# Moving one VectorE step ahead of a PSUM eviction in a modulated convolution kernel

## The chip, the cores and the metric

The kernel runs on one core of one Trainium2 chip. The metric is the device time of one execution in microseconds. The core's engines work side by side, each through its own queue in order: TensorE (PE, matmuls; its weight loads are listed as PEld), VectorE (DVE), ScalarE (ACT), GpSimd (POOL) and SyncE (SP, which issues most of the transfers). They wait for one another by semaphores.

## The reference

The input is x, 128 samples of 64 channels and 1024 positions, and a style vector of 128 numbers for each sample. Four convolution layers (64 to 64 channels, 3 taps) follow one another, each with weights of its own for each sample, and the result is added to x:

```python
TYPES = ('same', 'upsample', 'same', 'downsample')

def _layer(x, style, w, b, mw, mb, typ):
    s = style @ mw.T + mb
    weight = SCALE * w * s[:, None, :, None]
    demod = lax.rsqrt(jnp.sum(weight * weight, axis=(2, 3)) + EPS)
    weight = weight * demod[:, :, None, None]
    if typ == 'same':
        out = jax.vmap(_conv_same)(x, weight) + b[None, :, None]
    elif typ == 'upsample':
        out = jax.vmap(_conv_up)(x, weight.transpose(0, 2, 1, 3)) + b[None, :, None]
        out = _blur(out, 2.0 * blur_k, (1, 1))
    elif typ == 'downsample':
        xb = _blur(x, blur_k, (2, 2))
        out = jax.vmap(_conv_down)(xb, weight) + b[None, :, None]
    return out
...
out = x
for i, typ in enumerate(TYPES):
    out = _layer(out, style, weights[i], biases[i], mod_w[i], mod_b[i], typ)
return x + out
```

There is no nonlinearity between the layers, so for each sample the four of them are one convolution.

## The kernel before, in words

**Composing the taps.** The kernel doesn't run four layers over the data. For each sample it multiplies the four layers' weights into the nine taps of one convolution, and runs that over x. Samples come in groups of four; there are 32 groups, numbered q. The composition of one group is a chain of small matmuls with PSUM evictions between them:

- `scale3` (ScalarE) makes `wd`, the last layer's weights with the group's factors.
- Stage 1 (`stage1_a`, `stage1_b`) multiplies `wd` with the third layer's weights into the PSUM tile `psS`. ScalarE evicts one part into the SBUF tile S in `stage1_a`. In `stage1_b` VectorE evicts the rest with two instructions (line 481), and GpSimd then adds two slots of S (line 484). This is what "the eviction of S" means below: the two VectorE instructions.
- `share_sums` (VectorE), `share` (TensorE) and `share_copy` (ScalarE, line 529) prepare stage 2 of a group one turn ahead: three products that several taps have in common are made in a corner of another PSUM tile and copied into the PSUM tile `psR`.
- Stage 2 (`stage2_rest`, matmuls on line 506) adds the rest onto `psR`; ScalarE evicts it into R.
- Stage 3 makes the weights `Wf`; `combine_a` and `combine_b` (VectorE) make from them the weights H of a fast convolution.

`psS`, `psR` and the `psW` of stage 3 live in the pool `ps_w`, which has one buffer of two banks: each of them can be written only when the one before has been read.

**The convolution.** Three planes of x (each third position) make five data products, a fast convolution with five products in place of more. The inputs of the products are sums of planes: VectorE makes G from x in two steps, the third plane (`in_g2`, 684 elements a partition) and the first two planes (`in_g01`, 1376 elements); T1 and T2 are a sum and a difference of planes of G, made by GpSimd (`in1`, line 776, and `in2`, line 781); T04 (`in04`) and T3 (`in3`, line 761) are made by VectorE. TensorE's `conv0` to `conv4` multiply them with the weights into the PSUM tiles `psA` (two buffers) and Y; `sum1` and `sum2` (VectorE, which reads `psA` into y and writes Y) combine the products; `output` (ScalarE) scales, adds the bias and writes the tile o, which SyncE stores.

**The order.** It is written out by hand: each engine runs its instructions in the order in which the functions are called. A turn works on several groups at once: q is finished, n = q + 1 is in the middle of its convolution, c = q + 2 gets its inputs G, T1 and T3 and its stage 3, c + 1 its share, and s = q + 4 its stage 1. Turns 0 to 3 are `early_turn`, 4 to 28 are `turn_of`, and the last groups are written out singly. `sharing(q)` holds for q = 5 to 27.

`side(SIDE, q)` is work on the edges of the samples, spread over the turns: in most turns one VectorE instruction (as `add0`, `add2`, `blur_side`), in some several small ones (`setup0` in turn 10, `setup1` in 13, `setup3` in 15, `rest1_edges` in 18), and none in turns 14 and 19. `slot` is TensorE work on the edges, in turns 10, 14, 15 and 19.

Of the kernel before, what the change touches and what calls it, by code (L numbers as in the profile page):

```python
# [63 lines left out]
def kernel(  # L64
# [76 lines left out]
    def load(q, planes=slice(0, 3), cs=range(2)):  # L141

        if q < NQ:
            at = slice(planes.start * PL, planes.stop * PL)
            for c in cs:
                nc.sync.dma_start(Xs[q % NX][:, c, at], x[2 * q + c, :, at])
# [314 lines left out]
    def stage1_a(q, ps=None):  # L461

        ps = ps or unit(ps_w, f"psS{q}")
        wd = chain[q]
        tap_matmul(ps, wd, 2, 2, w2n[:, 0, :], EVEN, first=True)
        tap_matmul(ps, wd, 3, 2, w2n[:, 2, :], EVEN)
        tap_matmul(ps, wd, 1, 1, w2n[:, 1, :], slice(1, 2))
        st, t = s_tiles(q)
        for r in range(2):
            scaled_copy(nc_a, flat(st[r][:, :4]), ps[r][:, C : 5 * C], tBn[:, q, r : r + 1])  # L470
        chain[q] = wd, ps, st, t
# [88 lines left out]
    def stage2(q, pool=None, engs=(nc_a, nc_a), between=None):  # L560
        if q in shared_ps:
            ps = stage2_rest(q)
        else:
            ps = opened.pop(q, None)
            taps = range(9) if ps is None else range(3, 9)
            ps = stage2_taps(q, taps, ps or unit(pool or ps_w, f"psR{q}"))
        if between:
            between()
        t = r_pool.tile([P, 2, 9, C], F32, tag="R", name=f"R{q}")
        for r in range(2):  # L570
            scaled_copy(engs[r], flat(t[:, r, :7]), ps[r][:, : 7 * C], tC[:, q, r : r + 1])
        chain[q] = t
        return ps
# [62 lines left out]
    def r_sums(q, eng):  # L636
        t = chain[q]
        eng.tensor_add(t[:, :, 7:9], t[:, :, 2:6:3], t[:, :, 3:7:3])
# [3 lines left out]
    def stage3_b(q, ps):  # L642

        new_w(q)
        t = chain[q]
        plan = (
            (slice(0, 3), w0s[2][:, 2, :], slice(0, 7, 3)),
            (slice(0, 2), w0s[2][:, 1, :], slice(1, 5, 3)),
            (slice(0, 2), w0s[2][:, 0, :], slice(2, 6, 3)),
            (slice(3, 4), w0s[0][:, 0, :], slice(0, 1)),  # L650
            (slice(4, 5), w0s[1][:, 0, :], slice(1, 2)),
            (slice(4, 5), w0s[1][:, 1, :], slice(0, 1)),
            (slice(5, 7), w0s[0][:, 1, :], slice(7, 9)),
        )
        for i, (at, weight, slots) in enumerate(plan):
            same_row(blocks(ps, at), weight, t, slots, i == 0, i == len(plan) - 1)
        pw = shared_w[q] = unit(ps_w, f"psW{q}")
        src = blocks(ps, slice(5, 7))
        for i, f in enumerate((1.0, 1.0 / 3.0)):
            for dst, v in zip(blocks(pw, slice(i, i + 3, 2)), src):  # L660
                scaled_copy(nc_a, dst, v, f)
        stage3_out(q, ps, 0, 5)

    def stage3_a(q):

        t, pw = chain[q], shared_w.pop(q)
        plan = (
            (slice(0, 3, 2), Wd[:, 0], slice(3, 7, 3)),
            (slice(0, 3, 2), w0s[0][:, 2, :], slice(1, 5, 3)),
            (slice(1, 4, 2), Wd[:, 1], slice(2, 6, 3)),  # L670
            (slice(1, 2), w0s[1][:, 0, :], slice(4, 5)),
        )
        for i, (at, weight, slots) in enumerate(plan):
            same_row(blocks(pw, at), weight, t, slots, last=i == len(plan) - 1)
        stage3_out(q, pw, 5, 4)
# [35 lines left out]
    def sum_of(out, x, f, y, op=ALU.add):  # L711
        nc_v.scalar_tensor_tensor(out, x, f, y, op0=ALU.mult, op1=op)  # L712
# [6 lines left out]
    def combine_a(q):  # L719

        chain.pop(q)
        a, b, c, h1, h2, h3 = taps(q)
        sum_of(h1, c, -2.0, a)
        residual(q)
        sum_of(h3, h1, 1.0 / 6.0, b)

    def combine_b(q, steps=range(3)):

        a, b, c, h1, h2, h3 = taps(q)
        plan = (h2, c, -0.5, a), (h1, b, -3.0, h2, ALU.subtract), (h2, h2, -1.0 / 3.0, b)  # L730
        for i in steps:
            sum_of(*plan[i])
# [10 lines left out]
    def plane(buf, i, pairs=BOTH_PAIRS):  # L743

        at = PL * (2 - i) if i < 3 else PL * 2 + 1
        return buf[:, pairs, at : at + NJ]
# [6 lines left out]
    def g_tile(q):  # L753
        if q not in Gs:
            Gs[q] = gpool.tile([P, 2, 3 * PL], F32, tag="G", name=f"G{q}")
        return Xs[q % NX], Gs[q]
# [6 lines left out]
    def in_g01(q, pairs=BOTH_PAIRS):  # L763
        if q < NQ:
            X, g = g_tile(q)
            sum_of(g[:, pairs, PL:], X[:, pairs, : 2 * PL], 0.5, X[:, pairs, PL:], ALU.subtract)

    def in_g2(q, pairs=BOTH_PAIRS):
        if q < NQ:
            X, g = g_tile(q)  # L770
            sum_of(plane(g, 2, pairs), plane(X, 3, pairs), 0.5, plane(X, 2, pairs), ALU.subtract)
# [6 lines left out]
    def in2(q, eng):  # L778
        if q < NQ:
            t, g = t_tile(q, "T12"), Gs[q]  # L780
            eng.tensor_sub(t[:, :, 1, :NJ], plane(g, 2), plane(g, 1))  # L781
# [46 lines left out]
    def open_a(q):  # L828
        A[q] = ps_conv.tile([P, 2, 512], F32, tag="u", name=f"psA{q}")
        return banks(q)  # L830

    def conv3(q, pool=None):
        if pool:
            A[q] = unit(pool, f"psA{q}")
        elif q not in A:
            open_a(q)
        product(q, 3, banks(q))

    def copy_m3(q):
        m3c[q] = m_tile("m3", q)  # L840
        for s, a in parts(q):
            nc_a.copy(m3c[q][:, s], a)
# [10 lines left out]
    def conv2(q, *groups):  # L853
        product(q, 2, banks(q), groups or range(K))

    def sum2(q, steps=(0, 1)):
        if 0 in steps:
            m3 = m3c.pop(q)
            for s, a in enumerate(banks(q)):
                sum_of(Y[:, s, :NB], m3[:, s], 3.0, a[:, :NB])  # L860
        for s, a in parts(q) if 1 in steps else ():
            nc_v.tensor_sub(y1w[q][:, s], y1w[q][:, s], a)

    def conv4(q, *groups):
        product(q, 4, Y_banks, groups or range(K))

    def conv0(q, *groups):
        product(q, 0, banks(q), groups)
# [409 lines left out]
    def high(n):  # L1278
        return Y[:, 1, NB + 4 : NB + 4 + n]
# [84 lines left out]
    def side(work, q):  # L1364
        work.get(q, lambda: None)()
# [4 lines left out]
    def sharing(q):  # L1370
        return FIRST < q < NQ - 4
# [111 lines left out]
    def turn_of(q):  # L1483
        n, c, s = q + 1, q + 2, q + 4
        entry = q == FIRST
        stage2(c)
        if entry:
            sum2(q)
            conv4(q)
            combine_a(n)  # L1490
            r_sums(c, nc_v)
        else:
            conv2(q)
            r_sums(c, nc_g)
            sum2(q)
            in2(n, nc_g)
        side(TABLES, q)
        for i in range(3):
            load(c + 1, slice(i, i + 1))
        stage3_b(c, open_a(n))  # L1500
        if entry:
            conv0(q, 0, 1)
        else:
            combine_a(n)
            conv4(q)
        stage3_a(c)
        combine_b(n)
        conv3(n)
        if entry:
            copy_m3(n)  # L1510
            stage1_a(s)
        outputs(q, 2)
        if not entry:
            if s < NQ:
                stage1_a(s)
            copy_m3(n)
        in04(n)
        if sharing(q):
            share_sums(c + 1)
        in_g2(c)  # L1520
        side(SIDE, q)
        if q in SMALL:
            l, bs = SMALL[q]
            nc_v.memset(high(bs.stop - bs.start), 0.0)
        conv0(q, *((2,) if entry else range(K)))
        if entry:
            conv1(n, 0, 1)
        outputs(q, 1)
        if s < NQ:
            stage1_b(s)  # L1530
        in_g01(c)
        if sharing(q):
            share(c + 1, banks(q))
            share_copy(c + 1)
        outputs(q, 0)
        if q in SLOTS:
            matmuls, width, rest = SLOTS[q]
            slot(matmuls, width, Y_banks)
            rest()
        if s == NQ:  # L1540
            slot(ends3, 3, unit(ps_w, "psE"), 3)
            rest3()
        conv1(n, *((2,) if entry else range(K)))
        if q in SMALL:
            small(q)
        sum1(n)
        in3(c)
        side(LATE, q)
        if s == NQ:
            in04(c)  # L1550
        in1(c, nc_g)
        if s + 1 < NQ:
            scale3(s + 1)
# [6 lines left out]
    q, n, c = NQ - 3, NQ - 2, NQ - 1  # L1560
# [161 lines left out]
```

## Time and profile before

| what | value |
|---|---|
| median of three runs | 476.29 us (475.52 to 476.63) |
| span of the profiled execution, first to last instruction | 475.5 us |
| TensorE busy | 469.7 us, 99% |
| VectorE busy | 417.3 us, 88% |
| ScalarE busy | 312.0 us, 66% |
| GpSimd busy | 165.8 us, 35% |
| granted TensorE clock | 0.998 |

The profile gives the span as the profiled execution's own time; no other time of that execution is recorded. A page of the profile lists busy times, the span in slices, the DMA queues, the chain of waits that ended last, and groups of instructions. A row of the timeline reads: start in us from the span's start, duration in us (of all instructions of the row, where "x2" or more are merged), engine, line of the kernel, operation, tile written and tiles read, shapes, and in brackets the idle time of the engine before it with what ended that. A row of the waits reads: the waiting engine, tile and line, what it waited for, the total in us, how many times, the longest.

### The profile page before, as it was taken

To read this page: it belongs to the slowest core of one execution; us is meant where nothing else is said; L and a number is where in the kernel's file an instruction comes from. 1 tells how busy PE (TensorE), PEld (TensorE's weight loads), DVE (VectorE), ACT (ScalarE), POOL (GpSimd) and SP (SyncE) were. 2 spreads that over 40 slices of the span, in tenths; PEclk is the share of its full clock that TensorE was granted. 3 is DMA by queue.
4 is the path that set the end of the run, shared out by engine and by line. 5 is a ranking of instruction groups with operands and counts; after the bars stand their busy time and mean duration, and the time that the engine had idled before them with its cause. 6 is when DMAs were issued, how large, how long until landed. Compare 5 with 4: busy or idle time off the path is not lost.

```text
span 475.5 us, 26771 instructions
## 1 busy us (share of the span) xinstructions
PE 469.7 (99%) x11932; PEld 349.5 (74%) x11932; DVE 417.3 (88%) x694; ACT 312.0 (66%) x711; POOL 165.8 (35%) x200
## 2 busy tenths in 40 slices
PE   9999999999999999999999999999999999999996
PEld 6987788777678876677776677766788787876653
DVE  3889998879989998899979899979998999999896
ACT  4565657577766676766667666667666777766464
POOL 3634033664444342233432233422333423243200
PEclk9999999999999999999999999999999999999999
DMA  5237456535445554345544454543555544455225
GB/s 176 71 115 224 150 151 180 152 113 177 139 145 166 166 166 136 123 150 169 163 150 126 130 168 152 178 124 121 152 164 169 164 145 147 148 152 161 80 91 193
DMA packets 52707, 70.71 MB, mean 149 GB/s; under 512 B 6000, under 2 KB 50672, under 8 KB 52592
## 3 DMA queue, kind: packets, MB, share of 16 engines
q1 hardware_dynamic: 52368, 68.78, 46.3%
q8 instruction: 93, 1.52, 1.4%
q10 hardware_dynamic: 224, 0.22, 0.1%
q14 instruction: 22, 0.18, 0.1%
HBM read 35.36 MB, written 33.62 MB: 145 GB/s over the span
## 4 chain that ended last, share of the span: by engine, by line
PE 99%; DVE 0%; ACT 0%; issue 0%
PE psA L803 47%; PE Y L803 12%; PE psR L506 9%; PE psW L621 7%; PE psA L621 7%; PE psS L428 6%; PE psR L589 5%; PE psA L506 2%; PE Y L1044 2%; PE Y L183 1%; PE Y L379 1%; PE psM L220 0%; PE psE L1044 0%; PE Y L255 0%; DVE o L882 0%; PE psM L255 0%
## 5 line engine op out<-in xcount | busy, mean ns | idle before, releaser
L803 PE MATMUL psA<-T,H 64*64 64x340 f32 x2304 | 185.9, 446 | 0.0
L803 PEld LDWEIGHTS psA<-T,H 64*64 64x64 f32 x2304 | 90.7, 133 | 46.9 <-issue 2.5
L712 DVE SCALAR_TENSOR_TENSOR G<-X 128x1376 f32<-128x1376 f32 (+2 forms) x65 | 78.0, 1206 | 0.2
L776 POOL TENSOR_TENSOR T<-G 128x684 f32<-128x684 f32 x28 | 46.3, 1652 | 73.7 <-DVE G L712 73.7
L484 POOL TENSOR_TENSOR S<-S 128x128 f32<-128x128 f32 x28 | 21.6, 772 | 139.7 <-ACT S L399 139.6
L399 ACT ACTIVATE R<-psR,tC 128x448 f32<-128x448 f32 x63 | 36.6, 631 | 43.6 <-PE psR L506 25.8
L803 PE MATMUL psA<-T,Wf 64*64 64x340 f32 x768 | 63.7, 446 | 0.0
L803 PE MATMUL Y<-T,Wf 64*64 64x340 f32 x768 | 62.4, 451 | 0.0
L712 DVE SCALAR_TENSOR_TENSOR Y<-m,psA 128x340 f32<-128x340 f32 x62 | 32.0, 516 | 28.2 <-PE psA L803 26.9
L399 ACT ACTIVATE psW<-psA 128x128 f32<-128x128 f32 x100 | 19.3, 268 | 49.1 <-PE psA L621 45.0
L790 DVE TENSOR_TENSOR T<-G 128x1368 f32<-128x1368 f32 (+1 forms) x33 | 50.8, 1541 | 0.0
L399 ACT ACTIVATE Wf<-psW,t 128x256 f32<-128x256 f32 (+2 forms) x76 | 32.7, 480 | 26.7 <-PE psW L621 26.4
L761 DVE TENSOR_TENSOR T<-X 128x684 f32<-128x684 f32 x32 | 47.7, 1492 | 0.0
L506 PE MATMUL psR<-S,E 64*64 64x64 f32 (+1 forms) x1472 | 46.8, 237 | 0.0
L781 POOL TENSOR_TENSOR T<-G 128x684 f32<-128x684 f32 x28 | 46.5, 1660 | 0.0
L428 PEld LDWEIGHTS psS<-wd,w2n 64*64 64x64 f32 x1120 | 35.1, 133 | 12.9 <-issue 0.3
L506 PEld LDWEIGHTS psR<-S,E 64*64 64x64 f32 x1472 | 39.5, 134 | 4.9 <-ACT psR L529 0.2
L803 PEld LDWEIGHTS Y<-T,Wf 64*64 64x64 f32 x768 | 30.3, 132 | 16.8
L803 PEld LDWEIGHTS psA<-T,Wf 64*64 64x64 f32 x768 | 29.8, 133 | 14.5
L880 ACT ACTIVATE o<-psA,tb,td 128x340 f32<-128x340 f32 x63 | 37.1, 648 | 5.0 <-PE psA L803 2.8
L880 ACT ACTIVATE o<-y,tb,td 128x340 f32<-128x340 f32 x62 | 38.5, 678 | 0.0
L880 ACT ACTIVATE o<-Y,tb,td 128x340 f32<-128x340 f32 x62 | 36.1, 639 | 2.8 <-PE Y L803 2.0
(180 smaller groups left out, 840.4 us busy)
## 6 DMA issues: line engine op xcount, KB each, us to landing
out<-o SPq DMA_DIRECT2D x191, 170.0 KB, 2.6
X<-in_x SPq DMA_DIRECT2D x150, 172.0 KB, 3.4
X<-in_x SPq DMA_DIRECT2D x14, 516.0 KB, 5.0
par<-in_params SPq DMA_DIRECT2D x3, 192.0 KB, 3.8
Xe<-in_x_ends SPq DMA_DIRECT2D x1, 512.0 KB, 4.5
out<-Oe SPq DMA_DIRECT2D x2, 96.0 KB, 2.1
out<-o ACTq DMA_DIRECT2D x1, 170.0 KB, 2.8
par<-in_params SPq DMA_DIRECT2D x1, 160.0 KB, 2.7
```

Source lines behind the costliest of these rows:

```text
L399: nc_a.activation(dst, src, AF.Copy, scale=f)
L428: nc.tensor.matmul(ps[r][cols, at * C : (at + n) * C], weight[rows], wd[c if r == 0 else 1 - c][rows, taps], start=first, stop=last, skip_ ...
L506: nc.tensor.matmul(dst[r][cols], weight[rows], st[c if r == 0 else 1 - c][rows, slots, :], start=False, stop=last, skip_group_check=True,)
L589: nc.tensor.matmul(ps[r][cols, lo * C : (lo + m) * C], E[rows, e + 2, :], src[rows, a, :], start=(n == 0), stop=(n == 8), skip_group_check ...
L621: nc.tensor.matmul(dst[r][cols], weight[rows], t[rows, c, slots, :], start=first, stop=last, skip_group_check=True,)
L712: nc_v.scalar_tensor_tensor(out, x, f, y, op0=ALU.mult, op1=op)
L761: nc_v.tensor_sub(t[:, pairs, 0, :NJ], plane(X, 3, pairs), plane(X, 1, pairs))
L776: eng.tensor_add(t[:, :, 0, :NJ], plane(g, 2), plane(g, 1))
L781: eng.tensor_sub(t[:, :, 1, :NJ], plane(g, 2), plane(g, 1))
L790: nc_v.tensor_sub(t[:, pairs, :, :NJ], both(a, PL), both(b, 1))
L803: nc.tensor.matmul(ps[s][cols, :NB], w, Ts[q, tag][rows, c, i, g : g + NB], start=(g == 0 and (m == 3 or alone)), stop=(g == K - 1), skip_ ...
L880: nc_a.activation(dst, src, AF.Identity, bias=add, scale=d3)
```

## The change

In `turn_of` the call of `in_g01(c)` moves from behind `stage1_b(s)` to directly behind `in_g2(c)`. On VectorE this puts the instruction that makes the first two planes of G ahead of the turn's side work and of the two instructions that evict S. GpSimd's order stays as it was: its sum over S, then T1.

```diff
         if sharing(q):
             share_sums(c + 1)
         in_g2(c)
+        in_g01(c)
         side(SIDE, q)
         if q in SMALL:
             l, bs = SMALL[q]
...
         outputs(q, 1)
         if s < NQ:
             stage1_b(s)
-        in_g01(c)
         if sharing(q):
             share(c + 1, banks(q))
             share_copy(c + 1)
```

## The prediction

> **What bounds the kernel now.** I read the page first, then the waits, then the timeline of one turn engine by engine, and then the same few rows in all turns.
>
> ```profile
> span 475.5 us, 26771 instructions
> PE 469.7 (99%) x11932; PEld 349.5 (74%) x11932; DVE 417.3 (88%) x694; ACT 312.0 (66%) x711; POOL 165.8 (35%) x200
> PE 99%; DVE 0%; ACT 0%; issue 0%
> ```
>
> TensorE is busy for 99% of the span and carries the whole chain that ended last. So nothing is to be won by making another engine's work begin sooner: an edit can only leave TensorE alone or make it wait. The question is whether the step that is pushed back, the eviction of S, has enough cover. Who waits for whom around it, from the waits:
>
> ```profile
> ACT psR L529 <- DVE S L481: 1.0, 3, 0.6
> PEld psR L506 <- ACT psR L529: 0.2, 1, 0.2
> ```
>
> Both links exist and are already tight: in three turns ScalarE's copy into psR waits for VectorE's eviction of S (both use the same bank of ps_w), and once TensorE's next stage 2 waits for that copy. Now one turn (q = 12) on VectorE, from the Y eviction to the next one:
>
> ```profile
> 205.16 1.07 DVE L712 SCALAR_TENSOR_TENSOR Y<-m,psA 128x340 f32<-128x340 f32 x2 [0.97 <-PE psA L803]
> ...
> 211.86 0.87 DVE L712 SCALAR_TENSOR_TENSOR G<-X 128x684 f32<-128x684 f32 x1
> 212.64 0.81 DVE L1066 TENSOR_TENSOR Ye<-Ye,c 128x384 f32<-128x384 f32 x1
> 213.38 0.60 DVE L481 SCALAR_TENSOR_TENSOR S<-psS,tB,S 128x128 f32<-128x128 f32 x2
> 213.90 1.58 DVE L712 SCALAR_TENSOR_TENSOR G<-X 128x1376 f32<-128x1376 f32 x1
> 215.42 0.87 DVE L712 SCALAR_TENSOR_TENSOR y<-psA,m 128x680 f32<-128x680 f32 x1
> 216.21 1.81 DVE L761 TENSOR_TENSOR T<-X 128x684 f32<-128x684 f32 x1
> 219.00 1.07 DVE L712 SCALAR_TENSOR_TENSOR Y<-m,psA 128x340 f32<-128x340 f32 x2 [0.98 <-PE psA L803]
> ```
>
> VectorE waits once per turn, 0.98 us, for TensorE's conv2 ahead of the Y eviction. From there to the eviction of S it works without a break: the third plane of G (211.86), the side step (212.64), S (213.38), and only then the first two planes (213.90, the moved step). So each turn VectorE is put in step with TensorE at Y, and whatever is placed between Y and S delays S against TensorE in full. The other two engines in the same turn:
>
> ```profile
> 213.80 0.63 ACT L529 COPY psR<-psA 128x256 f32<-128x256 f32 x2
> ...
> 215.39 1.03 ACT L399 ACTIVATE wd<-w3x,tA 128x320 f32<-128x320 f32 x2
> 217.33 1.16 ACT L399 ACTIVATE R<-psR,tC 128x448 f32<-128x448 f32 x2 [0.91 <-POOL T L776]
> ```
>
> ```profile
> 213.38 1.90 PE L803 MATMUL psA<-T,H 64*64 64x340 f32 x24
> 215.10 0.40 PE L506 MATMUL psR<-S,E 64*64 64x128 f32 x8
> ```
>
> S ends at 213.98, the copies at 214.43 (0.45 later; the second copy follows the second half of S), and TensorE turns from conv1 to stage 2, which adds onto these copies, at 215.10. The slack of the eviction is 215.10 - 214.43 = 0.67 us.
>
> **The change, part by part.** Nothing is added or removed; one VectorE instruction per turn moves past the side step and the two S instructions. No DMA and no queue but VectorE's is touched. The moved step's inputs (X) were already being read by the third plane, so it has no new wait. From its start to the next start (213.90 to 215.42) it takes 1.52 us, and S comes 1.52 us later.
>
> What is behind S on VectorE: y1 and T3. y1 keeps its time, since the same work lies ahead of it, and conv1 (213.38 + 1.90) is done only just before it. Who waits for S: the two copies on ScalarE, and behind them two outputs, two wd and R. R waits for stage 2 anyway, and ScalarE is free 0.91 us before it, so ScalarE adds nothing of its own. Then TensorE: in turn 12 S ends at 215.50, the copies at 215.95, and stage 2 begins some 0.08 us behind them, at 216.03 instead of 215.10: **0.93 us of stall**. The 0.08 is my choice for the hand-over, between nothing and the 0.16 us from the end of G (213.90 + 1.58 = 215.48) to the POOL step that waits for it (215.64, below).
>
> The stall isn't made up later. TensorE has no idle time to give back, and the next Y waits for conv2, so VectorE's clock for the next turn starts late by the same amount. Each turn pays for itself.
>
> Now all turns. The share copies are made in the turns q = 5 to 27, 23 in all. The first and the last of them:
>
> ```profile
> 114.06 0.56 DVE L481 SCALAR_TENSOR_TENSOR S<-psS,tB,S 128x128 f32<-128x128 f32 x2
> 114.45 0.66 ACT L529 COPY psR<-psA 128x256 f32<-128x256 f32 x2
> 115.80 0.33 PE L506 MATMUL psR<-S,E 64*64 64x128 f32 x2
> ...
> 428.12 0.63 ACT L529 COPY psR<-psA 128x256 f32<-128x256 f32 x2
> ...
> 429.36 0.40 PE L506 MATMUL psR<-S,E 64*64 64x128 f32 x8
> ```
>
> Slack 0.69 in the first, 0.61 in the last. In the four turns 10, 14, 15 and 19 a group of matmuls for the ends stands between the share and conv1, and the slack is 2.1 to 3.3 us, more than 1.52. In the other 19 it lies between -0.04 (turn 18, the longest side step) and 0.69, with a mean of 0.54; VectorE goes through from the third plane to S in all of them. So the base is 19 x (1.52 + 0.08 - 0.54) = **20.1 us**. By the ends for the hand-over it is 18.6 (0) to 21.6 (0.16).
>
> **What the earlier T1 does.** It is read by the next turn's conv1, 13.84 us after the 213.38 above, and ends at 217.29 now: ten microseconds of cover, so its sooner start is worth nothing by itself. But it now lies beside the side step, and that matters:
>
> ```profile
> 87.13 0.46 POOL L484 TENSOR_TENSOR S<-S 128x128 f32<-128x128 f32 x1 [11.80 <-ACT S L399]
> 87.55 1.66 POOL L776 TENSOR_TENSOR T<-G 128x684 f32<-128x684 f32 x1
> 87.75 0.61 DVE L481 SCALAR_TENSOR_TENSOR S<-psS,tB,S 128x128 f32<-128x128 f32 x2 [1.28 <-PE psS L428]
> 188.52 0.86 DVE L761 TENSOR_TENSOR T<-X 128x684 f32<-128x684 f32 x1
> 212.21 0.82 POOL L484 TENSOR_TENSOR S<-S 128x128 f32<-128x128 f32 x1 [5.16 <-ACT S L399]
> 215.64 1.65 POOL L776 TENSOR_TENSOR T<-G 128x684 f32<-128x684 f32 x1 [2.61 <-DVE G L712]
> ```
>
> GpSimd's sum takes 0.46 us alone and 0.82 beside the third plane of G, ending 0.30 us after it (212.73 to 213.03): it stood until VectorE was done. T3 takes 0.86 us alone (188.52) and 1.81 beside T1, ending 0.73 us after it. So a VectorE step on two SBUF operands and a GpSimd sum exclude each other, an instruction at a time. The eviction of S, with one operand in PSUM, kept its 0.61 us right beside T1 (87.75).
>
> The Trainium skill has this in SBUF — State Buffer, section Who interferes with whom: the pair of ports that VectorE and GpSimd share is an exclusive lock, and whoever comes second is blocked for the whole instruction. The rows agree; by its rule the next sum is the base and the terms below, without it the base alone.
>
> T1 asks 0.16 us after the moved step ends, when the next VectorE step has begun already (starts overlap by 0.08). Where the side step is one instruction, T1 waits for it, and S is not touched: nothing. Where it is several, T1 gets in between and holds the rest for about 1.5 us (1.65 less the 0.15 that the lone 0.46 has above 0.30):
>
> ```profile
> 113.45 0.25 DVE L980 TENSOR_TENSOR cc<-Y,a 128x96 f32<-128x96 f32 x1
> 113.74 0.26 DVE L981 SCALAR_TENSOR_TENSOR cc<-b1s,cc 128x96 f32<-128x96 f32 x1
> 183.99 0.61 DVE L481 SCALAR_TENSOR_TENSOR S<-psS,tB,S 128x128 f32<-128x128 f32 x2
> 187.41 0.40 PE L506 MATMUL psR<-S,E 64*64 64x128 f32 x8
> 226.48 1.00 DVE L1016 SCALAR_TENSOR_TENSOR g<-par,g 128x192 f32<-128x192 f32 x2
> 256.78 0.61 DVE L481 SCALAR_TENSOR_TENSOR S<-psS,tB,S 128x128 f32<-128x128 f32 x2
> 259.97 0.41 PE L506 MATMUL psR<-S,E 64*64 64x128 f32 x8
> 299.06 1.39 DVE L1102 SCALAR_TENSOR_TENSOR Ue<-b1s,Ue 64x64 f32<-64x64 f32 x4
> ```
>
> Turn 18 (299.06, four steps): 1.5 us more. Turn 13 (226.48, two steps): the first is over about 0.28 us after G, the second ends 0.2 us after T1, at 1.98 instead of 0.65: 1.3 more. Turns 10 and 15 (setup0 and setup3, four small steps each): S is 1.52 + 1.45 = 2.97 us later; the slack, with S + 0.45 + 0.08, is 2.28 and 2.05, so 0.7 and 0.9 us of stall. Turns 5 and 6 have two steps, of which the first (113.45) reads PSUM and needs no lock; the second starts 0.21 us after the moved step's end against T1's 0.16, too close to tell. I count nothing there and keep 1.4 us each for the range. Sum: 20.1 + 1.3 + 1.5 + 0.7 + 0.9 = **24.5 us**.
>
> Elsewhere: in turn 4 S waits for ScalarE's output of Y, so the moved step fills idle time; in turn 28 no S is made. Both nothing. T3, of which T1 is now partly out of the way, gets up to 0.95 us shorter, and VectorE only waits longer for Y.
>
> **The rivals.** (1) The lock never falls between the side's steps, because back-to-back steps keep it: the base alone, 476.3 + 20.1 = 496.4. For it speaks that T1 asks when the next step is already queued; against it, that the side step of turn 12 took 0.81 us for 384 elements where T3 took 0.86 for 684, so GpSimd's sum did get in between two of them. (2) The lock also falls in turns 5 and 6: 500.8 + 2.8 = 503.6. (3) Not slower: VectorE, not TensorE, sets the turn, and a T3 that is 0.8 us shorter in 19 turns brings the next Y forward: 476.3 - 15 = 461. It decides only if Y is not waiting for TensorE, and the rows say it waits 0.98 us. A weaker form, in which S's readers have another 1 us of slack that I don't see, leaves 476.3; the two rows of waits speak against that.
>
> **How the numbers follow.** The trace's span is 475.5 us, the three runs have a median of 476.29; I add the 24.5 to the median: 500.8. Chances: this forecast 0.55, rival 1 0.2, rival 2 0.15, rival 3 in its two forms 0.05, anything else 0.05. The range takes in the first three cases with the ends of the hand-over: 476.3 + 18.6 = 494.9 down to a margin at 493.5, and 503.6 + 1.5 for the upper end, so 506. A change within 0.2% (1 us) is about what the measurement can't tell from none: 0.03; faster by more, 0.02; slower, 0.95.
>
> **What would show it.** In the changed profile the waits must have a large row of psR's weight loads for ScalarE's copy (some 20 us in about 20 turns) and one of that copy for S; TensorE's busy time must stay near 470 us while the span grows; turn 12 must last about 14.8 us; VectorE's wait for Y must grow to 2 us or more; turns 14 and 19 must keep their length. T1 must start about 1 us sooner relative to the third plane, and T3 be shorter. Turns 13 and 18 stalling by over 2 us show the lock; by about 1.1 and 1.6, rival 1. If TensorE shows no waits at stage 2, the reading of the slack is wrong.

## The result and the profile after

The changed kernel takes 503.84 us (median of four runs, 502.25 to 504.61) against 476.01 us before: 1.058 times as long, with an interval of 1.055 to 1.060. The forecast was 500.8 us, the range 493.5 to 506. The execution profiled after the change is the fastest of its four, 502.25 us at a granted clock of 0.998; the other three, at 0.994 to 0.995, took 503.42 to 504.61.

The page of the changed kernel: span; busy time by engine; the groups of the Y eviction and of stage 2 (line, engine, operation, count | busy us, mean ns of one | idle time before them and what ended most of it).

```profile
span 500.4 us, 26770 instructions
PE 478.8 (96%) x11932; PEld 359.8 (72%) x11932; DVE 410.1 (82%) x694; ACT 312.8 (63%) x711; POOL 169.3 (34%) x200
...
L712 DVE SCALAR_TENSOR_TENSOR Y<-m,psA 128x340 f32<-128x340 f32 x62 | 32.0, 516 | 64.1 <-PE psA L803 62.9
...
L506 PE MATMUL psR<-S,E 64*64 64x64 f32 (+1 forms) x1472 | 55.2, 241 | 12.8 <-ACT psR L529 12.7
```

VectorE works 7 us less than before and waits ahead of the Y eviction 64.1 us in all, 62.9 of it for TensorE's `psA`, which was 26.9 before. The matmuls of stage 2, which had no wait for ScalarE's copy into psR before (a weight load waited once, 0.2 us), now wait 12.7 us for it. The waits give the chain of it:

```profile
ACT psR L529 <- DVE S L481: 37.9, 20, 3.6
PEld psR L506 <- ACT psR L529: 24.4, 21, 3.2
PE psR L506 <- ACT psR L529: 12.7, 19, 2.6
PE Y L1295 <- DVE Y L1525: 2.7, 2, 1.4
```

The two links that stood at 1.0 and 0.2 us before are now at 37.9 and 24.4. (Matmuls and weight loads are listed apart; a wait of one overlaps with that of the other, so the two aren't added.) Turn 12 again, first on VectorE, then on GpSimd, ScalarE and TensorE:

```profile
219.39 2.36 DVE L712 SCALAR_TENSOR_TENSOR G<-X 128x684 f32<-128x684 f32 x2
221.68 0.81 DVE L1066 TENSOR_TENSOR Ye<-Ye,c 128x384 f32<-128x384 f32 x1
222.41 0.60 DVE L481 SCALAR_TENSOR_TENSOR S<-psS,tB,S 128x128 f32<-128x128 f32 x2
223.51 0.87 DVE L712 SCALAR_TENSOR_TENSOR y<-psA,m 128x680 f32<-128x680 f32 x1 [0.50 <-ACT psR L529]
224.29 0.86 DVE L761 TENSOR_TENSOR T<-X 128x684 f32<-128x684 f32 x1
227.44 1.07 DVE L712 SCALAR_TENSOR_TENSOR Y<-m,psA 128x340 f32<-128x340 f32 x2 [2.29 <-PE psA L803]
```

```profile
222.03 1.97 POOL L776 TENSOR_TENSOR T<-G 128x684 f32<-128x684 f32 x1
```

```profile
222.84 0.63 ACT L529 COPY psR<-psA 128x256 f32<-128x256 f32 x2 [0.88 <-DVE S L481]
```

```profile
221.47 1.90 PE L803 MATMUL psA<-T,H 64*64 64x340 f32 x24
223.25 0.60 PE L506 MATMUL psR<-S,E 64*64 64x128 f32 x6
```

The first row holds the third plane of G and the moved step, merged. S starts 3.02 us after the third plane (1.52 before), the copies follow it at once and end at 223.47. Stage 2's first matmul starts at 223.25, when the first of the two copies is in, 0.22 us ahead of the second copy's end; the matmuls that need the second copy start at 223.52. From the start of stage 2 to the next Y it is 4.19 us instead of 3.90. T1 starts 2.64 us after the third plane instead of 3.78, so the change does what it is for, and T3 takes 0.86 us instead of 1.81. TensorE's turn grew from 13.84 to 14.74 us all the same.

Turn by turn, from one start of stage 2 to the next (and in turn 5 from Y to stage 2), the change adds:

| turns | forecast, us | measured, us |
|---|---|---|
| 7 to 9, 11, 12, 16, 17, 20 to 27 | 15.5 | 13.8 |
| 13 and 18 | 2.8 + 2.8 | 5.5 |
| 10 and 15 | 1.6 | 1.4 |
| 5 and 6 | 1.8 | 4.4 |
| 14 and 19 | 0 | 0.6 |
| sum, 5 to 27 | 24.5 | 25.6 |

(The forecast's 20.1 of base is 15.5 and the 2.8 and 1.8 beside it.) The span grew by 24.9, 0.7 less, because in this trace the setup and the first turns, whose code is the same, were 1.1 us shorter, and what follows turn 27 was 0.4 us longer.

### The profile page after: what moved, and what is told of

Its sections match the earlier page's. It is cut to its first block, busy times and chain, and to the rows that moved or that the text cites. A ratio compares the mean times of both kernels' runs of the same rounds, so it can differ in the third digit from the quotient of the medians.

```text
span 500.4 us, 26770 instructions
## 1 busy us (share of the span) xinstructions
PE 478.8 (96%) x11932; PEld 359.8 (72%) x11932; DVE 410.1 (82%) x694; ACT 312.8 (63%) x711; POOL 169.3 (34%) x200
## 3 DMA queue, kind: packets, MB, share of 16 engines
q8 instruction: 93, 1.52, 1.4%
## 5 line engine op out<-in xcount | busy, mean ns | idle before, releaser
L803 PE MATMUL psA<-T,H 64*64 64x340 f32 x2304 | 188.6, 447 | 0.0
L803 PEld LDWEIGHTS psA<-T,H 64*64 64x64 f32 x2304 | 101.2, 133 | 38.5 <-issue 2.5
L712 DVE SCALAR_TENSOR_TENSOR Y<-m,psA 128x340 f32<-128x340 f32 x62 | 32.0, 516 | 64.1 <-PE psA L803 62.9
L712 DVE SCALAR_TENSOR_TENSOR G<-X 128x1376 f32<-128x1376 f32 (+2 forms) x65 | 81.8, 1296 | 0.2
L506 PE MATMUL psR<-S,E 64*64 64x64 f32 (+1 forms) x1472 | 55.2, 241 | 12.8 <-ACT psR L529 12.7
L506 PEld LDWEIGHTS psR<-S,E 64*64 64x64 f32 x1472 | 48.4, 133 | 26.4 <-ACT psR L529 24.4
L776 POOL TENSOR_TENSOR T<-G 128x684 f32<-128x684 f32 x28 | 50.1, 1791 | 44.8 <-DVE G L712 44.8
L803 PE MATMUL psA<-T,Wf 64*64 64x340 f32 x768 | 63.5, 446 | 0.0
L803 PE MATMUL Y<-T,Wf 64*64 64x340 f32 x768 | 62.3, 451 | 0.0
L399 ACT ACTIVATE R<-psR,tC 128x448 f32<-128x448 f32 x63 | 36.6, 631 | 26.9 <-PE psR L589 16.0
L781 POOL TENSOR_TENSOR T<-G 128x684 f32<-128x684 f32 x28 | 46.5, 1659 | 0.0
L638 POOL TENSOR_TENSOR R<-R 128x256 f32<-128x256 f32 x24 | 17.4, 726 | 83.7 <-ACT R L399 83.7
L428 PEld LDWEIGHTS psS<-wd,w2n 64*64 64x64 f32 x1120 | 34.2, 133 | 13.8 <-ACT o L880 0.9
L803 PEld LDWEIGHTS Y<-T,Wf 64*64 64x64 f32 x768 | 29.5, 132 | 17.2
L529 ACT COPY psR<-psA 128x256 f32<-128x256 f32 x46 | 14.6, 360 | 42.3 <-DVE S L481 37.9
L803 PEld LDWEIGHTS psA<-T,Wf 64*64 64x64 f32 x768 | 29.0, 133 | 15.0
L621 PEld LDWEIGHTS psA<-R,w0s 64*64 64x64 f32 x1000 | 39.0, 133 | 1.0
```

Of the source, the lines that this page charges most:

```text
L399: nc_a.activation(dst, src, AF.Copy, scale=f)
L428: nc.tensor.matmul(ps[r][cols, at * C : (at + n) * C], weight[rows], wd[c if r == 0 else 1 - c][rows, taps], start=first, stop=last, skip_ ...
L506: nc.tensor.matmul(dst[r][cols], weight[rows], st[c if r == 0 else 1 - c][rows, slots, :], start=False, stop=last, skip_group_check=True,)
L621: nc.tensor.matmul(dst[r][cols], weight[rows], t[rows, c, slots, :], start=first, stop=last, skip_group_check=True,)
L776: eng.tensor_add(t[:, :, 0, :NJ], plane(g, 2), plane(g, 1))
L803: nc.tensor.matmul(ps[s][cols, :NB], w, Ts[q, tag][rows, c, i, g : g + NB], start=(g == 0 and (m == 3 or alone)), stop=(g == K - 1), skip_ ...
```

## The experiments

Theory A is the prediction's: every microsecond put ahead of the eviction of S first uses up the turn's slack and is then paid by TensorE at stage 2, and T1 beside a side step of several instructions makes that longer. Theory B leaves the lock out, theory C puts the whole cost on T1 running beside the side step. The times are compared with the kernel before as it ran beside them: 476.03 us for one idle step, the side step behind T3 and one plane ahead, 475.57 us for the others. What single turns add is counted from the traces, as in the table above.

**The moved step behind the side step.** The moved step still stands ahead of S; only what T1 runs beside differs. The edit is shown against the changed kernel.

```diff
         in_g2(c)
-        in_g01(c)
         side(SIDE, q)
...
+        in_g01(c)
         if s < NQ:
             stage1_b(s)
```

> The moved step stands behind the side step and ahead of the eviction of S. Theory A (S comes 1.52 us later, and in turns 5, 6, 10, 13, 15 and 18 the T1 that is now beside the side step holds its later instructions as well): the eviction is as late, but T1 now falls beside S and y1, which read PSUM, so only the base is left. About 19.5 to 20 us over the kernel before, 496 us; turns 13 and 18 stall by 1.1 and 1.6 us instead of 2.4 and 3.0, turns 10 and 15 not at all. Theory B (the lock plays no part, those turns are slow for another reason of the order): as the changed kernel, 503.8 us. Theory C (the whole cost is T1 running beside the side step): as the kernel before, 476 us.

Measured: 495.81 us, 1.043 times the kernel before (1.040 to 1.045). Turn 18 in the changed kernel, VectorE, GpSimd and TensorE, and then the same turn of this run:

```profile
314.99 2.57 DVE L1102 SCALAR_TENSOR_TENSOR Ue<-b1s,Ue 64x64 f32<-64x64 f32 x4
317.59 0.61 DVE L481 SCALAR_TENSOR_TENSOR S<-psS,tB,S 128x128 f32<-128x128 f32 x2
```

```profile
315.24 1.63 POOL L776 TENSOR_TENSOR T<-G 128x684 f32<-128x684 f32 x1 [1.62 <-DVE G L712]
```

```profile
318.44 0.60 PE L506 MATMUL psR<-S,E 64*64 64x128 f32 x6 [2.57 <-ACT psR L529]
```

```profile
307.36 1.39 DVE L1102 SCALAR_TENSOR_TENSOR Ue<-b1s,Ue 64x64 f32<-64x64 f32 x4
308.78 1.59 DVE L712 SCALAR_TENSOR_TENSOR G<-X 128x1376 f32<-128x1376 f32 x1
310.29 0.60 DVE L481 SCALAR_TENSOR_TENSOR S<-psS,tB,S 128x128 f32<-128x128 f32 x2
```

```profile
310.54 1.66 POOL L776 TENSOR_TENSOR T<-G 128x684 f32<-128x684 f32 x1 [2.79 <-DVE G L712]
```

```profile
311.13 0.60 PE L506 MATMUL psR<-S,E 64*64 64x128 f32 x6 [1.12 <-ACT psR L529]
```

The four small steps take 2.57 us when T1 (315.24) comes between them and 1.39 when it doesn't. In the second order T1 (310.54) lies beside S, and S keeps its 0.60. Turn 18 adds 1.6 us here and 3.0 in the changed kernel, turn 13 1.1 and 2.4. Turns 5, 6, 10, 13, 15 and 18 together add 4.2 instead of 11.3, and the other fifteen 13.2 instead of 13.8. B and C fall; the lock is worth 7 to 8 us of the 27.8.

**Two idle VectorE steps ahead of S, without the change.**

```diff
+    def filler(q):
+        X, t = Xs[q % NX], t_tile(q, "T3")
+        sum_of(t[:, :, 0, :NJ], plane(X, 3), 0.5, plane(X, 2), ALU.subtract)
...
         in_g2(c)
+        filler(c)
+        filler(c)
         side(SIDE, q)
```

> The order of the kernel before, with two extra VectorE steps of 684 elements (their result is overwritten by T3) between the third plane of G and the side step. S comes 2 x 0.78 = 1.56 us later, T1 comes later too instead of sooner. Theory A: 19 x (1.56 + 0.08 - 0.54) = 20.9 us over the kernel before, 497 us, with TensorE waiting at stage 2 in 19 turns and no extra in turns 13 and 18. Theory C (the cost comes from T1 beside the side step): nothing, 476 us, since VectorE waits about 1 us per turn for conv2 and TensorE sets the time.

Measured: 501.59 us, 1.055 (1.053 to 1.057), 26 us instead of 20.9. C is out for good: here T1 comes later than before the change, and the cost is the same in kind, as the waits show:

```profile
ACT psR L529 <- DVE S L481: 39.0, 23, 2.3
PEld psR L506 <- ACT psR L529: 23.0, 19, 1.9
```

The size missed. VectorE in turn 12:

```profile
216.78 0.87 DVE L712 SCALAR_TENSOR_TENSOR G<-X 128x684 f32<-128x684 f32 x1
217.57 2.04 DVE L712 SCALAR_TENSOR_TENSOR T<-X 128x684 f32<-128x684 f32 x2
219.52 0.55 DVE L1066 TENSOR_TENSOR Ye<-Ye,c 128x384 f32<-128x384 f32 x1
219.99 0.60 DVE L481 SCALAR_TENSOR_TENSOR S<-psS,tB,S 128x128 f32<-128x128 f32 x2
```

The two take 1.95 us from the start of the first to the side step, 0.39 more than 2 x 0.78; the side step, which GpSimd's sum no longer holds, takes 0.55 us instead of 0.81. So S comes 1.69 us later behind the third plane and not 1.56. The formula with 1.69 gives 23.4, and the 19 turns add 22.2. Another 2.4 us came in turn 14, where VectorE, after turn 13's extra step, has no idle time ahead of Y and is late for it.

**One of them.** The same edit with one `filler(c)`.

> The order of the kernel before, with one extra VectorE step of 684 elements (overwritten by T3) between the third plane of G and the side step. S comes 0.78 us later; with the slack of each turn (0.35 to 0.69, -0.04 in turn 18) the formula of the prediction gives a stall of 0.17 to 0.51 us in 18 turns and 0.8 in turn 18, together 6.0 us; perhaps 1 us more in turn 14, where VectorE has least time left ahead of Y. Theory A: 6 to 7 us over the kernel before, 482 us. Two fillers cost 26, so if the cost were in proportion to the added work, without a slack to use up first, this would be 13 us, 489. Theory C (T1 beside the side step is the cost): 476 us.

Measured: 482.59 us, 1.015 (1.011 to 1.019), 6.6 us. One filler costs 6.6 and two cost 26: the first 0.54 us per turn are free and the rest is paid in full, as theory A has it; in proportion to the work it would be half of 26. In the seven turns with most slack (0.66 to 0.69 us: turns 5, 6, 7, 11, 12, 22 and 26) it added 0.1 us each on average; in turn 18, which has none, 0.9.

**T1 without its wait.** The order of the kernel before.

```diff
-            eng.tensor_add(t[:, :, 0, :NJ], plane(g, 2), plane(g, 1))
+            if 8 <= q < NQ - 1:
+                eng.memset(t[:, :, 0, :NJ], 0.0)
+            else:
+                eng.tensor_add(t[:, :, 0, :NJ], plane(g, 2), plane(g, 1))
```

> The order of the kernel before; in groups 8 to 30 GpSimd writes zeros into T1 instead of the sum of two planes of G, so that T1 doesn't wait for G at all and is done sooner than the change makes it, with S where it was. This leaves out that sum. Theory A: a sooner T1 is worth nothing, 476.0 us within 0.5, though T3 falls from 1.85 to 0.86 us and VectorE waits about 1 us longer per turn for conv2. Rival (a sooner T1, or the shorter T3 behind it, is worth time, which the change spent on S): faster by more than 1 us.

Measured: 475.97 us, 1.0004 (0.999 to 1.002). GpSimd, and VectorE's T3 and Y, in turn 12 (the kernel's lines behind the edit count three more here, L806 for L803):

```profile
212.15 0.83 POOL L484 TENSOR_TENSOR S<-S 128x128 f32<-128x128 f32 x1 [5.15 <-ACT S L399]
212.92 0.67 POOL L777 MEMSET T<- 128x684 f32 x1
```

```profile
216.14 0.86 DVE L761 TENSOR_TENSOR T<-X 128x684 f32<-128x684 f32 x1
218.94 1.07 DVE L712 SCALAR_TENSOR_TENSOR Y<-m,psA 128x340 f32<-128x340 f32 x2 [1.93 <-PE psA L806]
```

T1 is ready at 213.59, 3.7 us sooner than before (217.29), and T3 is 0.95 us shorter; VectorE waits 0.95 us longer at Y, and TensorE's turn keeps its length (13.85 us). What the change buys is worth nothing, even at no price.

**The side step behind S.** The changed kernel, with the side step moved in 14 turns.

```diff
+    LAST = {8, 9, 11, 12, 16, 17, *range(20, 28)}
...
         in_g01(c)
-        side(SIDE, q)
+        if q not in LAST:
+            side(SIDE, q)
...
             stage1_b(s)
+        if q in LAST:
+            side(SIDE, q)
```

> The changed kernel, with the side step of 14 turns (8, 9, 11, 12, 16, 17, 20 to 27) moved behind the eviction of S. In these turns S starts about 9.24 us after Y instead of 9.71 to 9.91, still about 1.1 us later than it can at the earliest. Theory A: a stall of 0.43 us in each of the 14 instead of 0.96 on average, so 7.3 us less than the changed kernel, about 496.5 us. Theory C (T1 beside the side step is the cost): the 14 turns keep their cost or lose it all, 503.8 or 490 us.

Measured: 500.13 us, 1.053 (1.050 to 1.055), a miss by 3.6 us. VectorE, GpSimd and TensorE in turn 12:

```profile
221.19 0.60 DVE L481 SCALAR_TENSOR_TENSOR S<-psS,tB,S 128x128 f32<-128x128 f32 x2
221.71 1.78 DVE L1066 TENSOR_TENSOR Ye<-Ye,c 128x384 f32<-128x384 f32 x1
223.41 0.85 DVE L712 SCALAR_TENSOR_TENSOR y<-psA,m 128x680 f32<-128x680 f32 x1
```

```profile
221.44 1.64 POOL L776 TENSOR_TENSOR T<-G 128x684 f32<-128x684 f32 x1 [1.62 <-DVE G L712]
```

```profile
224.41 0.80 PE L803 MATMUL psA<-T,H 64*64 64x340 f32 x8
```

S needs no lock, so T1 (221.44) took it first, and the side step behind S took 1.78 us instead of 0.55 alone. It now stands ahead of y1, y1 ends at 224.26, and conv2, which adds onto the bank that y1 reads, starts at 224.41, which is 2.39 us after the start of stage 2 instead of 2.09 in the changed kernel. The 14 turns add 8.2 us instead of 13.3, not the 6.0 expected.

**The side step behind T3.** The same, with the side step behind `in3(c)`, out of y1's way as well.

> The changed kernel, with the side step of the same 14 turns moved behind T3, so that it stands neither ahead of S nor ahead of y1. If the run with the side step directly behind S missed its number because T1 held the side step and y1 behind it, and TensorE's conv2 then waited for y1, that wait is gone here: a stall of 0.43 us in each of the 14 turns, 7.3 us less than the changed kernel, about 496.5 us. If the stall at stage 2 was mis-sized instead, it stays at 500.

Measured: 497.48 us, 1.046 (1.042 to 1.049). In turn 12 the side step takes 0.55 us there, and y1 waits for conv1 as it should:

```profile
224.05 0.87 DVE L712 SCALAR_TENSOR_TENSOR y<-psA,m 128x680 f32<-128x680 f32 x1 [0.68 <-PE psA L803]
224.83 0.86 DVE L761 TENSOR_TENSOR T<-X 128x684 f32<-128x684 f32 x1
225.61 0.55 DVE L1066 TENSOR_TENSOR Ye<-Ye,c 128x384 f32<-128x384 f32 x1
```

The 14 turns add 4.9 us, 0.35 each, and conv2 starts 2.10 us after stage 2 again. So what the 14 turns added beyond the 6.0 in the run before was y1 and conv2, and the stall at stage 2 was even a little smaller than the 0.43 expected. The rest of that run's miss lies in turn 14 of its trace, where TensorE's clock halves (see "Where TensorE's clock halves" below).

**One plane ahead, one behind.** The changed kernel, with only the plane that T1 needs ahead of the side step.

```diff
         in_g2(c)
-        in_g01(c)
+        in_g(c, 1)
         side(SIDE, q)
...
             stage1_b(s)
+        in_g(c, 0)
```

> The changed kernel, with only one of the two planes moved ahead of the side step (the one that T1 needs), the other left behind S. S comes 0.78 us later instead of 1.52, and T1 begins sooner still. Theory A: 6 us of base, and the lock's terms in turns 5, 6, 13 and 18 as in the changed kernel, 5.5 us; the second plane now meets T1 and may push y1 into conv2 by up to 0.3 us in 14 turns: 488 to 492 us. Without the lock: 482. If the cost went with how soon T1 begins, it would be more than the changed kernel's, over 504.

Measured: 491.13 us, 1.031 (1.027 to 1.035). Half the delay is 13 us less, although T1 begins sooner than in the changed kernel. The base and the lock add up as two separate terms: turns 5, 6, 13 and 18, where T1 still meets several steps, add 7.4 us, the 19 other turns together 6.2. No order tried here beats the kernel before.

## Why the prediction was right

**What bounds the kernel, and the stall.** Right: TensorE was never waiting, a sooner T1 bought nothing (475.97 us without T1's wait), and S with the copies into psR was the step without cover. The formula 1.52 + 0.08 - slack gave 0.93 us for turn 12, and 0.90 was measured; over the fifteen plain turns 15.5 against 13.8. Turn 7 makes up a quarter of that difference (0.49 instead of 0.9). There VectorE doesn't go through to S in the kernel before, as the prediction says of all 19 turns: its side step ends at 141.90 and S starts at 142.03, 0.11 us after the end of TensorE's last matmuls into `psS` (141.51, 0.41 us). In the changed kernel it has no such wait, so S comes only 1.27 us later behind Y, and not 1.49 as in turn 12.

Two steps of the picture were not as forecast, without effect on the number. The hand-over came out right only as a sum: stage 2 doesn't begin 0.08 us behind the copies but 0.22 us ahead of their end, and then loses 0.29 us up to the next Y. And y1 didn't keep its time: it waited 0.50 us, by the profile for the copies, and started 0.54 us later behind Y; conv2 starts 0.96 us after its end, so this cost nothing.

**The lock.** Right in kind, and in size for turns 13 and 18 (5.5 us against 5.6) and 10 and 15 (1.4 against 1.6; 0.4 of it remains where T1 isn't beside the side step, and the prediction has nothing there). The step that failed is the one on turns 5 and 6: "too close to tell. I count nothing there". VectorE, GpSimd and TensorE in turn 5 of the changed kernel:

```profile
112.35 1.85 DVE L712 SCALAR_TENSOR_TENSOR G<-X 128x1376 f32<-128x1376 f32 x1
114.13 0.25 DVE L980 TENSOR_TENSOR cc<-Y,a 128x96 f32<-128x96 f32 x1
114.41 1.68 DVE L981 SCALAR_TENSOR_TENSOR cc<-b1s,cc 128x96 f32<-128x96 f32 x1
116.11 0.14 DVE L1525 MEMSET Y<- 128x96 f32 x1
```

```profile
114.35 1.63 POOL L776 TENSOR_TENSOR T<-G 128x684 f32<-128x684 f32 x1 [1.60 <-DVE G L712]
```

```profile
116.30 0.38 PE L1295 MATMUL Y<-cc,wsum 64*64 64x96 f32 x4 [1.42 <-DVE Y L1525]
116.92 0.60 PE L506 MATMUL psR<-S,E 64*64 64x128 f32 x6 [0.24 <-ACT psR L529]
```

T1 asked at 114.35, 0.06 us ahead of the second step, and that one took 1.68 us instead of 0.26. The prediction had named the two starts 0.05 us apart, T1 first, and then not followed them. The term is 4.4 us instead of 1.8, 2.6 more. So rival 2 is the case that happened. That its 503.6 lies so close to the measured 503.84 is luck: the plain turns cost 1.7 us less than forecast and turns 14 and 19 0.6 more, so the turns add 25.6 us in the trace against 24.5. That is 1.1 of the 3.0 us by which the median is above the forecast, and another 1.6 lie between the profiled execution and the median. In turns 5 and 6 a memset of a corner of Y stands behind the side step as well, and a small matmul waits for it (the 1.42 us above) ahead of stage 2, a wait that the prediction hadn't seen; but stage 2 still waits for the copy after it, so S set the time here too.

**The other marks.** Y's wait grew to 2.3 and 2.7 us, T1 starts 1.1 us sooner and T3 is shorter, as forecast. TensorE's busy time was to stay near 470 us and came to 478.8: the matmuls of stage 2 went from 46.8 to 55.2 us of busy time at the same count, and in turn 12 the matmuls that need only the first copy run alone for 0.27 us (223.25 to 223.52), which counts as busy while the others wait for the second copy. Turns 14 and 19 were to keep their length and grew by 0.4 and 0.2.

**Where TensorE's clock halves.** Two traces hold turns that are 1.2 to 1.6 us longer than the same turns of the changed kernel, though nothing in the order explains it: turn 14 with the side step behind S, turns 6 and 19 with it behind T3. The page gives TensorE's granted clock in tenths over 40 slices of the span; here it is for the two runs:

```profile
PEclk9999999999999999999899999999999999999999
PEclk9999999998999999999999999899999999999999
```

The slices with an 8 hold stretches of 3.41 us at a granted clock of 0.50, from 238.73 us in the first run and from 118.81 and 316.78 us in the second, with 1.00 on both sides. They lie at these very turns, and none of them in the 14 turns that the two runs compare. The traces of the other runs have no such stretch before their last microseconds.

**What stays open.** Why the clock halves in some executions, why turns 14 and 19 grow a little, and a start that is up to 2.4 us shorter with the same code are not followed up.

## What to carry to other kernels

When one engine is busy all the time, look for what it will wait for next, not for what can begin sooner: measure the slack between the moved-back step and the first use of its result in each turn, and charge only what goes beyond it, but charge that in every turn. An in-order engine that is busy from its last wait to an eviction passes on every instruction put ahead of that eviction. Before two engines are brought side by side, check for each pair of neighbouring instructions whether they need the same port, and which asks first.

## What the runs showed of the hardware

A VectorE instruction on two SBUF operands and a GpSimd sum exclude each other for whole instructions, and GpSimd gets in between two VectorE instructions that follow one another without a break: four steps of 1.39 us took 2.57, and one of 0.26 took 1.68, when T1 came 0.06 us ahead of it. Evictions with one operand in PSUM kept their 0.60 us beside T1. The Trainium skill's page SBUF — State Buffer, section Who interferes with whom, has that second rule as well: a VectorE instruction with at most one SBUF input, outside what the page calls the 2-port perf modes, doesn't contend with GpSimd. The run with the moved step behind the side step agrees: S kept its 0.60 us beside T1 (310.29), and outside the lock's turns little changed (13.2 us against 13.8).

TensorE's granted clock fell to 0.50 for 3.41 us at a time in two of the traces, and the turn in which it did was 1.2 to 1.6 us longer, with no wait to show for it.
